# Planning the engine order of a two-layer vision kernel among 40 list schedulings, with refitted weights and DMA landing delays

## The chip, the cores and the metric

The kernel runs on one core of a Trainium2 chip. The metric is device microseconds (us) of one execution; a program on several cores would count its slowest. Its engines are TensorE (PE, matmuls; PEld is its weight load), VectorE (DVE), ScalarE (ACT), GpSimd (POOL) and SyncE (SP), which here only issues DMAs. Each works through its own instructions in order and waits for the others by semaphores.

## The reference

The input is x, (8, 192, 64, 64) in float32. Layer 0 is a windowed attention block, layer 1 a Fourier mixer with an MLP:

```python
# layer 0, windows of 8 x 8 pixels, 6 heads of 32
shortcut = layer_norm(xs)                        # over the 192 channels
q, k, v = split(windows(shortcut) @ qkv_w.T + qkv_b)
attn = einsum(l2n(q), l2n(k)) * temperature      # 64 x 64 per window and head
kth = top_k(attn, 16)[0][..., -1:]
attn = softmax(where(attn >= kth, attn, -100) + rpb)
x2 = shortcut + unwindow(attn @ v) @ proj_w.T + proj_b
x2 = x2 + gelu(layer_norm(x2) @ fc1_w.T + fc1_b) @ fc2_w.T + fc2_b
# layer 1
f = fft2(layer_norm(x), norm="ortho")            # per channel, 64 x 64
h = gelu([f.real, f.imag] @ fc1_w.T + fc1_b) @ fc2_w.T + fc2_b
x = x + ifft2(complex(h[0], h[1])).real
out = x + gelu(layer_norm(x) @ mlp1_w.T + mlp1_b) @ mlp2_w.T + mlp2_b
```

## The kernel before, in words

An image (batch) is cut into 8 bands of 512 pixels. The work is written as Python generators, called tasks, one for each piece:

- `front(b, i)`: loads a band (`load_band`, two bands ahead), turns it into token form on PE (`lt`), normalizes, turns it back (`lc`), makes q, k (`pq`) and v (`pv`) and the norms of q and k (POOL power, L771).
- `attention(b, i, hb)`, two per band: scales q and k, scores on PE (`s`, L924), the 16 largest of each row on DVE (L952 to L956), the mask, softmax over POOL, ACT and DVE, then the transposition of the weights. In batch 0 PE does that (`turned_by_pe`); from batch 1 on DVE transposes 32 x 32 blocks and four SP writes to DRAM (L889) and one SP load (L892) do the rest (`turned_by_dma`). Then the product with v on PE (`po`, L997).
- `back(b, i)`: projection (`pp`), residual, and the first MLP (`mlp`): statistics, normalization (`normalized`, L530 on ACT or L535 on DVE), transposition (from batch 1 on by DVE, four SP writes L580 and three SP loads L583 and L585 into `hn`), first product (`mh`, L622 and L635), gelu on ACT (L606), second product (`mo`, L668).
- `forward`, `pointwise`, `inverse`, for each group of 16 channels: the Fourier transform in matmuls (`fa`, `fz`), the pointwise MLP (`fh` L1177, gelu L1160, `fo` L1204) and the transform back (`fb`, `fy`).
- `leave(b, j)`: the second MLP and the store.

A task yields an `op` before each step: the engine, or a choice of engines (`EITHER` is ACT or DVE), an estimated time for each in units of 10 ns, the tile mode of PE or the table of ACT, buffers that it takes (`get`) and gives back (`put`), and what it waits for (`after`). The function `issue` (L33) is a list scheduler. It keeps, while the program is built, a clock for each engine and a time for each free buffer. The tasks lie in streams (`streams`, at the end of the kernel function): 6 for setup, then `front` with 1 task open at a time, `attention` 3, `back` 2, `forward` 1, `pointwise` 2, `inverse` 1, `leave` 2. At each turn `issue` computes the earliest begin for every open task's next step, takes for each engine the step with the smallest `begin + cost + 360 * place - 100 if it frees PSUM` among those that can begin within 15 units of the first, and issues the one of all engines that begins earliest. `place` is the due place of the task in batches. A change of PE's mode costs 20, of ACT's table 130. A result counts on another engine 15 units later, from PE 30, from SP 210; on the same engine at once. DVE is taken in a choice only if it ends 40 earlier than ACT. The instructions of the step are emitted at that moment, so that the order of choices is the order on each engine and on SP's queue. There are 4 PSUM buffers, 7 `h`, 5 `att`, 4 `xt`, 2 `hn`, 3 each of the DRAM buffers `rows` and `turn`.

The lines that set the old clock:

```python
change = {"pe": 20, "act": 130, "dve": 0, "pool": 0, "sp": 0}
arrives = {"pe": 30, "sp": 210}
...
                    if source is not None and source != engine:
                        end += arrives.get(source, 15)
```

Two steps whose weights the prediction uses are `yield op("sp", 220, put="att")` ahead of the four writes of L889 (and of L580), and `yield op("sp", 45, get="att", put="turn")` ahead of the load L892; the loads of `hn` have 130.

Of the kernel before, what the change touches and what calls it, by code (L numbers as in the profile page):

```python
# [28 lines left out]
def op(engine, weight, mode=None, get="", put="", after=None, done=None, put_too=""):  # L29
    return engine, weight, mode, get.split(), (put + " " + put_too).split(), after, done  # L30


def issue(streams, units):  # L33

    change = {"pe": 20, "act": 130, "dve": 0, "pool": 0, "sp": 0}
    arrives = {"pe": 30, "sp": 210}
    clock = {e: 0 for e in change}  # L40
    mode = {e: None for e in change}
    units = {name: [0] * n for name, n in units.items()}
    events = {}
    live = []

    def advance(task, value):
        try:
            found = task["gen"].send(value)
            while not isinstance(found, tuple):

                new = dict(task, gen=found, queue=None)
                live.append(new)
                advance(new, None)
                found = task["gen"].send(None)
            task["op"] = found
        except StopIteration:
            live.remove(task)
            if task["queue"] is not None:
                start(task["queue"])

    def start(queue):
        if queue[0]:
            gen, place = queue[0].pop(0)
            task = {"gen": gen, "queue": queue, "urgency": 360 * place, "last": (None, 0)}
            queue[1] += 1
            task["order"] = (queue[1], len(live), place)
            live.append(task)
            advance(task, None)

    for tasks, width in streams:  # L70
        queue = [list(tasks), 0]
        for _ in range(width):
            start(queue)
    while live:
        best, ready = {}, {}
        for task in live:
            engines, weights, kind, get, put, after, done = task["op"]
            if isinstance(engines, str):
                engines, weights = (engines,), (weights,)
            free = 0  # L80
            deps = [task["last"]] if after is None else after
            deps = [d if d[0] is None or d[0] in change else events.get(d) for d in deps]
            if any(d is None for d in deps):
                continue
            short = False
            for name in set(get):
                n = get.count(name)
                if len(units[name]) < n:
                    short = True
                    break  # L90
                free = max(free, sorted(units[name])[n - 1])
            if short:
                continue
            found = []
            for engine, weight in zip(engines, weights):
                begin = max(clock[engine], free)
                for source, end in deps:
                    if source is not None and source != engine:
                        end += arrives.get(source, 15)
                    begin = max(begin, end)  # L100
                new = kind and mode[engine] and kind != mode[engine]
                cost = change[engine] if new else 0
                found.append((begin + cost + weight, engine, begin, cost, task, weight))

            _, engine, *rest = min(found, key=lambda f: f[0] + 40 * (f[1] == "dve"))
            ready.setdefault(engine, []).append((engine, *rest))
        for engine, found in ready.items():
            first = min(begin + cost for _, begin, cost, *_ in found) + 15
            best[engine] = min(
                [  # L110
                    (
                        begin + cost + task["urgency"] - 100 * ("ps" in task["op"][4]),
                        task["order"],
                        f,
                    )
                    for f in found
                    for _, begin, cost, task, _ in [f]
                    if begin <= first
                ],
                key=lambda v: v[:2],  # L120
            )
        choice = min(best.values(), key=lambda v: (v[2][1], v[:2]))[2]
        engine, begin, change_cost, task, weight = choice
        _, _, kind, get, put, after, done = task["op"]
        for name in get:
            units[name].remove(min(units[name]))
        end = begin + change_cost + weight
        clock[engine] = end
        if kind:
            mode[engine] = kind  # L130
        for name in put:
            units[name].append(end + (150 if engine == "sp" else 15))
        task["last"] = (engine, end)
        if done:
            events[done] = (engine, end)
        advance(task, (engine, end))


@with_exitstack
def kernel(  # L140
# [7 lines left out]

# [66 lines left out]
    make_identity(nc, ident)  # L225
# [274 lines left out]
    def statistics(src, nm):  # L500
# [3 lines left out]
        for j in range(2):  # L504
            yield op("dve", 54 + 42 * j)
            for t in range(2):
                nc.vector.bn_stats(st[:, t, j, :], src(t, j))
# [5 lines left out]
    def normalized(to, pair, src, mv, nm):  # L513

        yield op("pool", 130)
# [8 lines left out]
        for j in range(2):  # L524
            done = yield op(EITHER, (72, 96), after=[shifted])
# [32 lines left out]
    def mlp(src, nm, w1, fc1_bias, w2, by_dma, then=None):  # L558
# [7 lines left out]
        if by_dma:  # L566
            ready = yield op("dve", 115, get="att rows", put="xa", after=last)
# [7 lines left out]
            yield op("sp", 220, put="att")  # L575
# [5 lines left out]
            yield op("sp", 130, get="hn", put="rows")  # L581
# [7 lines left out]
        else:  # L589
# [3 lines left out]
            done = yield op(EITHER, (80, 96), put="ps")  # L593
# [4 lines left out]
        def gelu(fp, ph, last):  # L598
            yield op("act", 138, "gelu", put="ps", after=[last], done=("gelu", nm, fp))
# [59 lines left out]
        for half in range(2):  # L659
            if half == 0:  # L660
                yield op("pe", 384, "full", get="ps", after=last)
                acc = psum(f"mo_{nm}")
            else:
                last = yield op("pe", 384, "full", put="h h h")
# [16 lines left out]
    def front(b, i):  # L681
# [16 lines left out]
        done = yield op(EITHER, (80, 96), put="ps")  # L698
# [13 lines left out]
        for part in range(2):  # L712
            weights = (100, 100) if part else (62, 67)
# [29 lines left out]
        def squares(p, pq):  # L743
            copied = yield op(EITHER, (80, 96), put="ps")
            copy(copied, qk[:, :, p, :], pq[:, :, : 2 * C])
            squared = yield op(("act", "pool"), (81, 150), get="xa")
# [5 lines left out]
            yield op("dve", 95, put="xa", done=("sq", b, i, p))  # L752
# [23 lines left out]
        def values(whole):  # L776
            done = yield op(EITHER, (80, 96), put="ps", after=[whole], done=("vv", b, i))
            copy(done, vv.rearrange("p t a c -> p t (a c)"), pv[:, :, : 2 * C])
# [77 lines left out]
    def turned_by_pe(s, nm):  # L856
# [11 lines left out]
        moved = yield op(EITHER, (80, 96), put="ps")  # L868
# [4 lines left out]
    def turned_by_dma(s, nm):  # L873
# [3 lines left out]
        yield op("dve", 108, get="att turn", put="att")  # L877
# [6 lines left out]
        yield op("sp", 220, put="att")  # L884
# [16 lines left out]
    def attention(b, i, hb):  # L901

        nm = f"{b}_{i}_{hb}"
        scaled = yield op(("pool", "dve"), (195, 140), after=[("front", b, i, hb), "rpb"])
# [13 lines left out]
        yield op("pe", 55, "s", get="ps ps att", put="qkt")  # L918
# [13 lines left out]
        for k in range(2):  # L932
            done = yield op(EITHER, (49, 56), put="ps")
# [9 lines left out]
        for k0 in range(0, 12, 2):  # L943
            yield op("dve", 100, get="sm" if k0 == 0 else "")
# [12 lines left out]
        yield op("dve", 106)  # L957
        mask = small(shape, "mask", U8)
        nc.vector.tensor_tensor(mask, s, top[:, :, :, 15:16].to_broadcast(shape), ALU.is_lt)
        yield op("dve", 108)  # L960
        nc.vector.copy_predicated(s, mask, row(neg.unsqueeze(1).to_broadcast([128, 3, 4])))  # L961

        yield op("pool", 150)
        nc.gpsimd.tensor_tensor(s, s, top[:, :, :, 0:1].to_broadcast(shape), ALU.subtract)  # L964
        yield op("pool", 190)
        nc.gpsimd.tensor_tensor(s, s, rpb.unsqueeze(2).to_broadcast(shape), ALU.add)
        yield op("act", 85, "exp")
        nc.scalar.activation(s, s, AF.Exp)
        yield op("dve", 117)
# [3 lines left out]
        yield op("pool", 150, put="sm")  # L973
# [7 lines left out]
        if hb == 0:  # L981
            yield op("pe", 53, "v", get="ps ot", put="att", after=[moved, ("vv", b, i)], done=("ot", b, i))
            ots[b, i] = strip("ot", 2, f"ot_{nm}")
        else:
            yield op("pe", 53, "v", get="ps", put="att " + held[b, i][1], after=[moved, ("ot", b, i)])
# [18 lines left out]
        done = yield op(EITHER, (72, 72), put="ps", done=("att", b, i, hb))  # L1004
# [10 lines left out]
    def back(b, i):  # L1015
# [28 lines left out]
        yield op("dve", 98, put="ps", after=[last, ("xt", b, i)])  # L1044
# [5 lines left out]
        def biased():  # L1050
            yield op("pool", 183, done=("biased", b, i))
# [5 lines left out]
        if i > 0:  # L1057
# [3 lines left out]
            98,  # L1061
# [19 lines left out]
        yield op("pool", 200, done=("in", b, i))  # L1081
# [9 lines left out]
    def forward(b, n):  # L1091

        nm = f"{b}_{n}"
        yield op("pool", 250, get="xf", after=[("in", b, i) for i in range(NB)] + ["layer1"])
# [9 lines left out]
        yield op("pe", 90, "full", get="ps fa", put="xf")  # L1104
# [9 lines left out]
        yield op("dve", 70, put="ps")  # L1114
# [11 lines left out]
        yield op("pe", 100, "row32", get="ps ps fz", put="fa")  # L1126
# [13 lines left out]
        for k in range(2):  # L1140
            yield op("dve", 43 + 33 * k, put="ps", done=("fz", b, n) if k else None)
# [10 lines left out]
    def pointwise(b, n, half):  # L1152
# [4 lines left out]
        def gelu(hf, k, ph):  # L1157
            yield op("act", 111, "gelu", put="ps", done=("fh", nm, hf, k))
# [3 lines left out]
        for hf in range(2):  # L1162
            yield op(
                "pe",
                86,
# [21 lines left out]
        if half == 1:  # L1187
# [3 lines left out]
            172,  # L1191
# [142 lines left out]
    with tc.manual_schedule():  # L1334
        issue(streams, units)
# [80 lines left out]
```

## Time and profile before

| | us |
|---|---|
| runs shown (three) | 4822.05, 4823.49, 4830.06; median 4823.49 |
| the profiled execution, its own time | 4827.91 |
| its span, first to last instruction | 4826.1 |
| mean granted clock of PE | 0.963 |
| ACT busiest line: L1160, gelu of the pointwise MLP, 768 times | 813.3 |
| DVE: L952, L954, L956, the search of the 16 largest | 255.8, 309.5 and 125.2, 265.3 |
| POOL busiest line: L771, a power, 128 times | 557.1 |
| DMA moved | 246.42 MB, 51 GB/s on average |

Busy times are unions of the instructions' spans. "a <- b" in a list of waits reads: engine, tile and line that waited, then what ended the wait, the time in total, the number of waits and the longest. SPq is the queue of SP. In a group, "busy, mean ns of one" stand ahead of the bar, idle time of the engine after it. The chain that ended last is put to 66% on PE, 10% on DVE, 7% on POOL, 7% on DMA, 5% on ACT.

### The profile page before, as it was taken

The numbers are of one execution on the slowest core, as the hardware profiler recorded it, in microseconds if no ns is written. First come the engines' busy times: TensorE is split into PE (matmuls) and PEld (weight loads), VectorE is DVE, ScalarE is ACT, GpSimd is POOL, SyncE is SP. The second block draws the span as 40 slices with busy tenths as digits, with TensorE's granted clock in tenths as the row PEclk, the third lists the DMA queues.
The fourth block names the chain that finished last, engine by engine and source line by source line (L and its number), as shares of the span: only waits on it lengthen the run. The fifth ranks groups of instructions, "written<-read, shape, count | busy, mean of one in ns | idle before, by whom it ended". The sixth has DMA issues, their size and how long they took to land.

```text
span 4826.1 us, 143829 instructions
## 1 busy us (share of the span) xinstructions
PE 4441.2 (92%) x60506; PEld 3512.4 (73%) x60506; DVE 2695.8 (56%) x10965; ACT 2542.1 (53%) x3769; POOL 2358.2 (49%) x2188
## 2 busy tenths in 40 slices
PE   6787998999999999899999999999989999999989
PEld 5675766876778766687677876787767877778758
DVE  6776655546665555646665546646476565662111
ACT  4455655346564556445564455644566355652553
POOL 6667545345554455444554455545465465551200
PEclk7888999999999999999999999999999999999999
DMA  2001111221123111222112211122111221121002
GB/s 57 11 8 37 54 32 54 72 61 48 37 59 85 53 41 44 61 73 57 42 46 72 70 48 41 54 67 80 31 48 46 78 70 38 54 63 53 13 15 66
DMA packets 271072, 246.42 MB, mean 51 GB/s; under 512 B 39983, under 2 KB 223482, under 8 KB 270426
## 3 DMA queue, kind: packets, MB, share of 16 engines
q1 hardware_dynamic: 270414, 237.22, 17.7%
q8 instruction: 476, 7.80, 0.7%
q14 instruction: 170, 1.39, 0.1%
q10 hardware_dynamic: 12, 0.00, 0.0%
HBM read 120.52 MB, written 116.39 MB: 49 GB/s over the span
## 4 chain that ended last, share of the span: by engine, by line
PE 66%; DVE 10%; POOL 7%; DMA 7%; ACT 5%; issue 3%; SPq 2%; DVEq 0%; ACTq 0%; POOLq 0%
PE mo_d L668 8%; PE mo_b L668 7%; PE mh_b L622 7%; PE mh_d L622 6%; PE fh L1177 6%; PE fo L1204 6%; PE mh_b L635 3%; PE mh_d L635 3%; PE pq L787 3%; POOL nrm L771 3%; DMA at<-ar 3%; ACT fh L1160 2%; DMA ar<-tt 2%; PE fy L1252 2%; PE fb L1225 2%
## 5 line engine op out<-in xcount | busy, mean ns | idle before, releaser
L1160 ACT ACTIVATE fh<-fh,ab 128x1024 f32<-128x1024 f32 x768 | 813.3, 1110 | 347.0 <-PE fh L1177 344.7
L771 POOL TENSOR_TENSOR nrm<-nrm,mhalf 128x24 f32<-128x24 f32 x128 | 557.1, 4352 | 10.7
L964 POOL TENSOR_TENSOR s<-s,top 128x768 f32<-128x768 f32 x128 | 191.5, 1496 | 720.6 <-DVE s L961 559.5
L668 PE MATMUL mo_b<-wfc,h_b 128*128 128x192 f32 x3072 | 520.5, 328 | 1.0 <-ACT fh L1160 0.5
L668 PE MATMUL mo_d<-wmlp,h_d 128*128 128x192 f32 x3072 | 515.5, 328 | 0.0
L668 PEld LDWEIGHTS mo_b<-wfc,h_b 128*128 128x128 f32 x3072 | 497.8, 190 | 17.4 <-issue 10.7
L668 PEld LDWEIGHTS mo_d<-wmlp,h_d 128*128 128x128 f32 x3072 | 500.5, 190 | 12.7 <-issue 9.6
L1177 PE MATMUL fh<-fz,w1p 32*128 32x264 f32 (+1 forms) x6144 | 468.6, 410 | 14.7 <-ACT fh L1160 6.5
L622 PE MATMUL mh_b<-hn_b,wfc_a 128*128 128x256 f32 x1536 | 391.3, 402 | 34.8 <-DMA hn_b<-lr_b 20.3
L1177 PEld LDWEIGHTS fh<-fz,w1p 32*128 32x128 f32 x6144 | 295.3, 189 | 149.9 <-issue 84.3
L1204 PE MATMUL fo<-fh,w2p 128*32 128x264 f32 (+1 forms) x6144 | 390.9, 389 | 5.7 <-ACT fh L1160 5.5
L622 PE MATMUL mh_d<-hn_d,wmlp_a 128*128 128x256 f32 x1536 | 371.1, 390 | 25.8 <-DMA hn_d<-lr_d 23.1
L622 PEld LDWEIGHTS mh_b<-hn_b,wfc_a 128*128 128x128 f32 x1536 | 290.6, 197 | 109.8 <-issue 42.0
L606 ACT ACTIVATE h_d<-mh_d,fcb 128x512 f32<-128x512 f32 x384 | 240.8, 686 | 230.5 <-PE mh_d L635 169.8
L622 PEld LDWEIGHTS mh_d<-hn_d,wmlp_a 128*128 128x128 f32 x1536 | 286.8, 193 | 88.2 <-issue 44.1
L974 POOL TENSOR_TENSOR s<-s,rsum 128x768 f32<-128x768 f32 x128 | 193.9, 1517 | 241.8 <-DVE rsum L972 157.4
L954 DVE MATCH_REPLACE8 s<-top,s 128x64 f32<-128x64 f32 x1536 | 309.5, 209 | 0.0
L1204 PEld LDWEIGHTS fo<-fh,w2p 128*32 128x32 f32 x6144 | 185.3, 111 | 165.3 <-issue 40.0
L952 DVE MAX8 top<-s 128x8 f32<-128x64 f32 x1536 | 255.8, 207 | 70.4 <-ACT s L852 70.0
L606 ACT ACTIVATE h_b<-mh_b,fcb 128x512 f32<-128x512 f32 x384 | 241.3, 690 | 81.9 <-PE mh_b L635 59.4
L1290 DVE TENSOR_TENSOR zt<-mo_d,xy 128x768 f32<-128x768 f32 x64 | 61.3, 957 | 380.1 <-PE mo_d L668 380.1
L956 DVE MAX8 top<-s 128x8 f32<-128x64 f32 x1536 | 265.3, 214 | 0.0
(214 smaller groups left out, 8469.0 us busy)
## 6 DMA issues: line engine op xcount, KB each, us to landing
ar<-tt SPq DMA_DIRECT2D x448, 96.0 KB
at<-ar SPq DMA_DIRECT2D x112, 384.0 KB
lr_d<-lt_d SPq DMA_DIRECT2D x256, 96.0 KB
lr_b<-lt_b SPq DMA_DIRECT2D x224, 96.0 KB
xin<-in_x SPq DMA_DIRECT2D x64, 256.0 KB
hn_d<-lr_d SPq DMA_DIRECT2D x64, 256.0 KB
out<-z SPq DMA_DIRECT2D x64, 256.0 KB
hn_b<-lr_b SPq DMA_DIRECT2D x56, 256.0 KB
```

The source lines that it names most:

```text
L606: nc.scalar.activation(to, of, AF.Gelu, bias=fc1_bias[:, 2 * fp + k : 2 * fp + k + 1],)
L622: nc.tensor.matmul(ph[:, t, k * HALF : (k + 1) * HALF], w1[0][:, f], hn[:, t * HALF : (t + 1) * HALF], start=(first and k == 0), stop=not ...
L635: nc.tensor.matmul(ph[:, t, k * HALF : (k + 1) * HALF], w1[1][rows, f], hn[rows, BAND:ROW], start=(first and k == 0), stop=not first, skip ...
L668: nc.tensor.matmul(acc[:, j, t * C : (t + 1) * C], hs[f // 2][:, f % 2, q * 128 : (q + 1) * 128], w2[:, f, ORDER[t]], start=(f == 0 and t ...
L771: nc.gpsimd.tensor_tensor(nf, nf, mhalf[:, :24], ALU.pow)
L952: nc.vector.max(best[:, 0:8], of)
L954: nc.vector.match_replace(s2, best[:, 0:8], of, -3.0e38)
L956: nc.vector.max(best[:, 8:16], s2)
L974: nc.gpsimd.tensor_tensor(s, s, row(rsum), ALU.mult)
L1160: nc.scalar.activation(hs[hf, k], ph, AF.Gelu, bias=ab[:, 0:1])
L1177: nc.tensor.matmul(phs[k // 2][:, k % 2, cols], w1p[i][rows, hf].rearrange("p h v -> p (h v)"), fz[rows, :] if rhs is None else zu[rows, : ...
L1204: nc.tensor.matmul(po[rows, :] if i == 0 else pou[rows, :, 1 : U - 1], w2p[i][:, hf].rearrange("p a v -> p (a v)"), hs[hf, k // 2][:, k % ...
```

## The change: what it does

The scheduler is split. `program` builds tasks; the kernel calls it first with a dummy (`Mute`) that swallows every instruction, and `listed` runs all tasks through once, in order of place, and notes for each step its engines, weights, buffers and predecessors. `Plan` then schedules this list with the old rules (same key, the same 15 units, the same 40 on DVE, the same places), and `search` does it in steps: from each state it runs 40 schedules over 40 us, the first without noise, the others with a normal noise of 25 units (0.25 us) added to each step's key; the one with the most work (PE's time counted in full, that of other engines by 0.15) is run for 20 us, and so on. The real program is then issued in the order found. A task may no longer pass the one before it in its stream at the same step (`front`). The clock's constants and the weights are set anew, and a step on SP that follows one on SP now waits for 145.

```diff
-    change = {"pe": 20, "act": 130, "dve": 0, "pool": 0, "sp": 0}
-    arrives = {"pe": 30, "sp": 210}
+CHANGE = {"pe": 19, "act": 128, "dve": 0, "pool": 0, "sp": 0}
+ARRIVES = {"pe": 22, "dve": 18, "act": 15, "pool": 11, "sp": 265}
...
+    def wake(self, task):
...
+            for d in waits:
+                source = self.engine[d]
+                end = self.end[d] + (ARRIVES[source] if source != engine else 145 * (source == "sp"))
+                if end > begin:
+                    begin = end
...
+    def run(self, until, noise=None):
...
+                a = front[task]
+                if a is not None and at[a] <= at[task]:
+                    continue
...
+                        end = begin + cost + weight + (40 if engine == "dve" else 0)
...
+                    key = begin + cost + place[task] - (100 if "ps" in put else 0)
+                    if noise:
+                        key += noise(number)
...
+    def search(self, tries=40, step=2000, horizon=4000, spread=25):
+        draw = random.Random(1)
+        now = 0
+        while self.ready:
+            now = max(now, self.clock["pe"])
+            kept, best = self.save(), None
+            for k in range(tries):
+                seed = draw.random()
+                noise = drawn(seed, spread) if k else None
+                if not self.run(now + horizon, noise):
+                    self.restore(kept)
+                    continue
+                worth = 0
+                for _, _, engine, begin, weight in self.log[kept[-1]:]:
+                    part = min(weight, max(0, now + horizon - begin))
+                    worth += part if engine == "pe" else 0.15 * part
+                if not self.ready:
+                    worth = 1e9 - max(self.clock.values())
+                if best is None or worth > best[0]:
+                    best = worth, seed if k else None
+                self.restore(kept)
+            seed = best[1]
+            self.run(now + step, drawn(seed, spread) if seed is not None else None)
+            now += step
...
+def issue(streams, plan):
+    tasks = Tasks(streams)
+    for name, engine, number in plan:
+        tasks.advance(name, (engine, number))
...
+    streams, units = program(Mute(), Mute(), x, out, w)
+    ops, of_task, made = listed(streams, units)
+    plan = Plan(ops, of_task, made, units, [width for _, width in streams]).search()
+    streams, _ = program(ctx, tc, x, out, w)
+    with tc.manual_schedule():
+        issue(streams, plan)
```

The weights that were changed and matter most, in units of 10 ns:

| step | before | after |
|---|---|---|
| copies out of PSUM, 768 wide, ACT or DVE | 80 or 96 | 69 or 87 |
| normalization, two instructions, ACT or DVE | 72 or 96 | 89 or 58 |
| gelu L1160, one instruction | 111 | 100 |
| gelu L606, two instructions | 138 | 115 |
| scaling of q and k, POOL or DVE | 195 or 140 | 148 or 98 |
| two rows of the search of the 16 largest, DVE | 100 | 90 |
| copies of `po`, ACT or DVE | 72 or 72 | 42 or 54 |
| statistics, first half, DVE | 54 | 50 |
| POOL steps of the softmax | 150, 190, 150 | 157, 177, 144 |
| half of `mo`, PE | 384 | 390 |
| scores `s`, product `po`, PE | 55, 53 | 61, 62 |
| four writes on SP | 220 | 200 |
| loads of `hn` on SP | 130 | 100 |

The computation, its instructions apart from the choices of engine, the buffers and the streams stay.

## The prediction

> **What bounds the kernel now.** I read the page's busy table first, then the windows of 200 us, then the waits of PE by stretch, then those of SP, then single lines and a piece of the timeline.
>
> ```profile
> PE 4441.2 (92%) x60506; PEld 3512.4 (73%) x60506; DVE 2695.8 (56%) x10965; ACT 2542.1 (53%) x3769; POOL 2358.2 (49%) x2188
> ```
>
> PE is the bound. No other engine is above 56%, so the order of work matters only by what it does to PE: its idle time (4826.1 - 4441.2 = 385 us) and what is wasted inside its busy time. The windows tell where the idle time lies (columns: window, its length, busy us of PE, PEld, DVE, ACT, POOL with instructions, PE clock, DMA share, GB/s).
>
> ```profile
> 0.00:200.00 200.00, 140.65 (x1504) 104.75 (x1505) 140.48 (x596) 85.26 (x148) 129.35 (x117) 0.79 0.17 38
> 200.00:400.00 200.00, 162.70 (x1806) 132.24 (x1806) 145.46 (x674) 102.03 (x178) 145.84 (x126) 0.86 0.05 12
> ...
> 1800.00:2000.00 200.00, 171.76 (x2933) 125.49 (x2926) 123.10 (x518) 112.89 (x155) 104.31 (x92) 0.93 0.15 42
> 2000.00:2200.00 200.00, 197.60 (x1690) 172.72 (x1690) 109.72 (x464) 85.69 (x144) 85.09 (x85) 0.99 0.26 72
> ```
>
> The first 400 us lose 97 us; there only batch 0's attention and first MLP exist, and DVE and POOL, at 70%, feed PE. The full stretches lose 2 to 28 us in 200. Summed from the trace by what ended each PE wait: 118 us before 600 us, 227 us from 600 to 4400, 29 us after. Of the 227, DMA ended 119.5, ACT 40.6, DVE 37.0, the sequencer ("issue") 27.7, others 2.2. The waits of PE in that middle stretch:
>
> ```profile
> PE po L997 <- DMA at<-ar: 92.2, 49, 4.6
> PE mh_b L622 <- DMA hn_b<-lr_b: 17.4, 10, 4.6
> PE fb L1235 <- issue: 14.8, 15, 1.6
> PE mh_d L622 <- DMA hn_d<-lr_d: 9.9, 8, 2.6
> ```
>
> So half of PE's idle time in the body is spent behind two matmuls whose operand SP still has on its way (49 waits of 1.88 us, 18 of 1.52 us). PE is in order, so everything planned behind them stands too. That the planner thinks SP faster than it is shows in SP's own waits:
>
> ```profile
> SPq L892 <- DMA ar<-tt: 164.7, 192, 3.2
> SPq L583 <- DMA lr_d<-lt_d: 106.7, 100, 3.5
> SPq L583 <- DMA lr_b<-lt_b: 92.4, 86, 3.1
> ```
>
> The load waits for the landing of the write that stands right before it, which the old planner prices at nothing, since both are on SP.
>
> **The change, part by part** (planner units are 10 ns: half an output product is 24 matmuls, whose usual start-to-start in the trace is 163 ns, 3.91 us; weights 384 and now 390).
>
> (a) Landing delays. Old chain from the transposed tile to `po`: write 220, load 45, arrival 210: 4.75 us. New: 200 + 145 + 45 + 265 = 6.55 us, 1.80 later. For `hn`: 220 + 130 + 210 = 5.60, now 200 + 145 + 100 + 265 = 7.10, 1.50 later. The trace's waits above are 1.88 and 1.52: the correction is almost exactly the error. The records behind it: SP released 1.46 us after the last write's issue ended (24 cases), `po` 2.86 us after its load's (53), `mh` 2.39 after its load's (22). If PE has something else ready for these slots, the waits of L997 and L622 go: 92.2 + 17.4 + 9.9, with 6.9 of `po` before 600 us and 2.9 after 4400, 129 us. If nothing is ready, PE idles just as long: 0. Up to 12 tasks of seven streams (and their sub-tasks) are open at a time and PE was busy in 94% of the middle, so I take three quarters: -95. What is late next is the `ACT` and `DVE` group, 78 us. What stands behind a load on SP (writes of other tasks, `xin` loads, `out`) now waits by plan, not by surprise; SP issues for only 919 us in all, so I count nothing there.
>
> (b) Weights. The timeline shows what they now count:
>
> ```profile
> 2610.21 3.58 ACT L606 ACTIVATE h_d<-mh_d,fcb 128x512 f32<-128x512 f32 x6
> ```
>
> Six activations in 3.58 us are 0.597 each, though their mean is 0.686 in the groups: one begins before the last has ended. The pair weight goes from 138 to 115. Likewise the 128x1024 gelu, 1.110 in the groups and 1.011 from start to start, goes from 111 to 100, and copies from 80 to 69 (0.695 start to start). The new set agrees with start-to-start times within some 2%, the old with durations. A truer clock means fewer PE instructions placed before their operand or after it. Of the 78 us on ACT and DVE I take a quarter, -20. Bounds: -60 and +40 (tighter plan, those waits grow by half).
>
> (c) Choice among 40 schedules. Each 20 us step is tried 40 times over 40 us with noise of 0.25 us on the keys, and the one with the most PE work (0.15 of the others') is kept. Changes of PE tile mode are no work, so they lose. I count 2,018 in the trace's order of matmuls. Across one, start to start is about 0.306 us; usual steps are 0.216 (256 columns), 0.163 and 0.109, so one costs 0.09 to 0.20, and I take 0.14, the 192-column step, the commonest: 283 us in all. A tenth fewer gives -28, rounded to -30. Bounds: +14 (5% more) and -70 (a quarter fewer).
>
> (d) The first 600 us, 118 us of idle, 50 of it POOL: `at` behind `s` 48.6 us. Here latency bounds, not order, but which of three attentions goes first is order. I take -20; bounds +20 and -60 (half).
>
> (e) Normalizing weights go from ACT 72, DVE 96 to 89, 58; with DVE's handicap of 40 it is now taken when ACT is 9 units late (before 64). Today 522 of 768 run on ACT. Should 200 more go, DVE gains 200 x 0.29 = 58 us beside its 2696, ACT loses 200 x 0.44 = 88: hidden under PE. But these are the ones that POOL can hold up:
>
> ```profile
> L535 DVE TENSOR_SCALAR xa_b<-xt,mv_b,rs_b x86: 306/374/1981, 172.3 to 4428.7; 128x192 f32<-128x192 f32 x86
> ```
>
> Of 246 such instructions 19 took 0.74 to 1.98 us, each lying over one POOL instruction to its end: an extra 1.2 us each, 19/246 x 200 x 1.2 = 19 us more on DVE, unplanned. On PE's path I count 0, at worst +15. The Trainium skill's GPSIMD Engine Reference, section 1 (Specifications), speaks against this shift: GpSimd shares SBUF interfaces with VectorE and contends with its two-port instructions. By it each of the 200 could meet POOL, busy 49%, at 1.2 us each, 118 us of DVE; the rows show 8%, not 49%, so the sum stays with the rows.
>
> (f) A later task of a stream may no longer overtake an earlier one at the same step: 0; it only fixes the order that the places already give.
>
> **Sum**: -95 - 20 - 30 - 20 = -165. Against the profiled execution, 4827.9 (span 4826.1 and 1.8 around it): 4662.9. The median of the runs, 4823.5, lies 4.4 lower: **4659**. All bounds together would give 4504 (-319) to 4912 (+89).
>
> **Rivals.**
>
> *Nothing fills the slots.* The new plan puts `po` 1.8 us later and PE idles by plan instead of by wait, because its other work hangs on the same chains. For it: 1800 to 2000 us loses 28 us with DVE, ACT and POOL at 62% or less, so there PE lacked ready work. Against: 2000 to 2200 loses 2.4. With (a) at a quarter, -32, and (c) at half, -15, and the rest: 4737. It holds 4715 to 4813.
>
> *The search finds more.* It also picks schedules by what they make of whole stretches. Should PE idle in the middle halve (-114), the start give -60 and a quarter of the mode changes go (-70): 4823 - 244 = 4580. The granted clock would help: 0.93 where 28 us were idle, 0.99 where 2.4 were. The Trainium skill's TensorE: Matmul & The Clock Gate, Part 1, has the clock halved after about 3.4 us without work; the waits of (a) are shorter, so by the page filling them raises no clock. It holds below 4600.
>
> *Slower: the plan has no slack left.* The old weights put some 0.1 us of reserve on each ACT and DVE result: `fo` was planned 1.11 + 0.15 after its gelu began, now 1.00 + 0.15, and the gelu takes 1.11 by itself, 0.04 of margin. All engines are in order, so each small miss (a POOL collision, a granted clock under 1) stands on PE. By the code there are some 2,970 planned PE steps; a mean extra stall of 0.08 us gives +238, less the 95 of (a) and 50 of (c) and (d): +93, 4916. It decides from 145/2970 = 0.05 us per step. Against it: `fh` behind `ACT fh` waits 0.36 us, but 16 times in 384, and stalls shift later work too, so they don't add one to one. It holds above 4833.
>
> *The plan does not do what it says.* The order is fixed by the planner's clock; if the chip strays from it by more than the noise of 0.25 us within one 40 us horizon, the choice among 40 is a lottery and only (a) and (b) are left: 4823 - 115 = 4708. That lies at the edge of the forecast and is counted half there, half with the first rival.
>
> **Chances.** Forecast (4600 to 4715) 0.50; nothing fills 0.21; more 0.14; within 0.2% 0.04; slower 0.11. 0.2%, some 10 us, is about what a measurement of this kernel can tell from no change. Faster by more 0.85, same 0.04, slower 0.11. The range leaves out the slower case and the lower half of the third (0.07): **4575 to 4813**.
>
> **What would show each step.** (a): `po` behind `DMA at<-ar` falls from 99.1 us under 40 in all, and `mh` behind `hn` under 20. If those fall and PE's busy share stays at 92%, the first rival holds. (b): PE waits on ACT and DVE under 78 us in the middle; above 120 the slower rival holds. (c): fewer than 1,900 changes of tile mode, and PE's busy time below 4441. (d): the first 600 us of the windows more than 481 us busy. (e): more than 246 at L535's successor, with some of them over 1.2 us. The prediction is wrong if PE's idle time moves into waits that no SP chain has, or if the whole program only gets through the start faster.

## The result, and the profile after

The changed kernel takes 4669.61 us (median of 4 runs, 4656.83 to 4674.24) against 4826.77 for the kernel before beside it: a ratio of 0.967, 95% interval 0.9648 to 0.9693, 157 us less. 4659 was predicted. The profiled execution took 4674.24, its span is 4672.5, 153.6 less than before's.

The page's busy table, and the same windows as before (PE, PEld, DVE, ACT, POOL, PE clock, DMA share, GB/s):

```profile
PE 4401.0 (94%) x60506; PEld 3481.1 (75%) x60506; DVE 2738.3 (59%) x11037; ACT 2515.1 (54%) x3704; POOL 2364.3 (51%) x2195
```

```profile
0.00:200.00 200.00, 139.81 (x1570) 105.26 (x1570) 145.55 (x632) 83.53 (x148) 133.42 (x116) 0.81 0.17 39
200.00:400.00 200.00, 181.28 (x2074) 148.98 (x2072) 155.41 (x700) 112.92 (x199) 166.46 (x146) 0.95 0.07 19
...
1800.00:2000.00 200.00, 193.13 (x2810) 148.79 (x2808) 126.54 (x525) 119.56 (x167) 119.54 (x107) 0.99 0.21 59
2000.00:2200.00 200.00, 195.00 (x1852) 166.30 (x1852) 95.09 (x382) 80.23 (x131) 61.13 (x70) 0.98 0.23 65
```

PE has the same 60,506 matmuls, is busy 40 us less and idle 113 us less. The second window does 2,074 of them where it did 1,806, and its clock is 0.95, not 0.86. PE's waits from 600 to 4400 us, and SP's own:

```profile
PE po L1181 <- DMA at<-ar: 22.6, 16, 3.4
PE mh_d L806 <- DMA hn_d<-lr_d: 17.9, 16, 2.3
...
PE fb L1419 <- issue: 6.1, 6, 1.6
...
PE mh_b L806 <- DMA hn_b<-lr_b: 4.0, 5, 1.2
```

```profile
SPq L1076 <- DMA ar<-tt: 124.0, 136, 3.4
...
SPq L767 <- DMA lr_b<-lt_b: 84.6, 83, 3.3
...
SPq L767 <- DMA lr_d<-lt_d: 56.5, 73, 2.8
```

`po` waited 92.2 us here and now 22.6, `mh` 27.3 and now 21.9. SP still waits for the landings, 265 us against 364: that wait is still there, but PE stands behind it less often.

**Where PE's 40 busy us went.** The clock records have two values, full and half, and the pieces at half are 3.4 us long or a multiple of it, but for the last one. Before, the clock stood at half for 354 us, 254 of them with PE busy; after, for 207 and 145. Work at half clock takes twice its time (neighbouring products of L622 start 0.427 us apart there and 0.216 at full clock, medians in the kernel before), so 109 us less of it saves 55. Taking half of the busy time at half clock off gives PE's busy time at full speed: 4314 before, 4329 after, and 4319 to 4343 in the twelve kernels below. So everywhere the span is some 4330 + idle time + half of the busy time at half clock. For the change: -113 idle, -55 clock, +14 rest.

How a short wait costs clock can be seen in the timeline of PE in the kernel before:

```profile
2138.69 1.46 PE L622 MATMUL mh_d<-hn_d,wmlp_a 128*128 128x256 f32 x6
2142.41 1.04 PE L997 MATMUL po<-at,vv 64*32 64x64 f32 x64 [2.26 <-DMA at<-ar]
2143.38 3.21 PE L622 MATMUL mh_d<-hn_d,wmlp_a 128*128 128x256 f32 x8
```

and, of the same kernel, eight matmuls of the same shape without a wait ahead of them:

```profile
2652.48 1.89 PE L622 MATMUL mh_b<-hn_b,wfc_a 128*128 128x256 f32 x8
```

PE stands 2.26 us behind `at`; the clock goes to half 0.06 us after that wait and stays there for 3.41 us. The eight products take 3.21 us where 1.89 is usual, so the wait cost 2.26 us and 1.32 us on these products.

### The profile page after: what moved, and what is told of

Same layout as the page of the kernel before. It is cut to its first block, busy times and chain, and to the rows that moved or that the text cites. A ratio compares the mean times of both kernels' runs of the same rounds, so it can differ in the third digit from the quotient of the medians.

```text
span 4672.5 us, 143843 instructions
## 1 busy us (share of the span) xinstructions
PE 4401.0 (94%) x60506; PEld 3481.1 (75%) x60506; DVE 2738.3 (59%) x11037; ACT 2515.1 (54%) x3704; POOL 2364.3 (51%) x2195
## 5 line engine op out<-in xcount | busy, mean ns | idle before, releaser
L852 PE MATMUL mo_b<-wfc,h_b 128*128 128x192 f32 x3072 | 530.4, 331 | 9.5 <-issue 7.3
L852 PEld LDWEIGHTS mo_b<-wfc,h_b 128*128 128x128 f32 x3072 | 504.0, 192 | 24.0 <-issue 13.6
L806 PE MATMUL mh_b<-hn_b,wfc_a 128*128 128x256 f32 x1536 | 379.9, 392 | 13.4 <-ACT hn_b L1036 4.0
L701 POOL TENSOR_SCALAR rs_d<-mv_d 128x4 f32<-128x4 f32 x64 | 15.4, 240 | 574.9 <-DVE mv_d L694 555.3
L1136 DVE MAX8 top<-s 128x8 f32<-128x64 f32 x1536 | 256.2, 208 | 65.7 <-ACT s L1036 65.5
```

The source lines that it names most:

```text
L806: nc.tensor.matmul(ph[:, t, k * HALF : (k + 1) * HALF], w1[0][:, f], hn[:, t * HALF : (t + 1) * HALF], start=(first and k == 0), stop=not ...
L852: nc.tensor.matmul(acc[:, j, t * C : (t + 1) * C], hs[f // 2][:, f % 2, q * 128 : (q + 1) * 128], w2[:, f, ORDER[t]], start=(f == 0 and t ...
L1136: nc.vector.max(best[:, 0:8], of)
```

## The experiments

Ratios are to the kernel before on the same chip. Per profiled execution: PE's idle time, its busy time at half clock, and its waits behind `at` and `hn`, all in us. A plan made without the search is called plain here.

| kernel | ratio (95%) | idle | half clock | `at` | `hn` |
|---|---|---|---|---|---|
| before | 1 | 385 | 254 | 99 | 43 |
| the change | 0.967 (0.9648 to 0.9693) | 271 | 145 | 33 | 37 |
| landing_only | 0.9784 (0.9763 to 0.9805) | 292 | 166 | 15 | 38 |
| plain_old | 0.9971 (0.9959 to 0.9984) | 358 | 217 | 54 | 38 |
| plain_free | 0.9969 (0.9958 to 0.9979) | 355 | 205 | 54 | 34 |
| no_search | 0.9912 (0.9894 to 0.9929) | 351 | 198 | 74 | 46 |
| no_landing | 0.9793 (0.977 to 0.9815) | 304 | 160 | 73 | 45 |
| seed2 | 0.9703 (0.9681 to 0.9724) | 271 | 104 | 30 | 38 |
| old_weights | 0.9637 (0.9617 to 0.9657) | 262 | 118 | 52 | 39 |
| old_seed2 | 0.9626 (0.9605 to 0.9647) | 254 | 119 | 29 | 50 |
| chain_old | 0.9566 (0.9543 to 0.9588) | 226 | 108 | 9 | 26 |
| sp_reserve | 0.9619 (0.9604 to 0.9634) | 246 | 98 | 7 | 28 |
| norm_old | 0.9625 (0.961 to 0.964) | 236 | 103 | 16 | 32 |
| chain_norm | 0.9635 (0.9619 to 0.9652) | 259 | 130 | 21 | 54 |

Theory A was the prediction's: the landing delays carry most of the gain. Theory B: the search does. Theory C: the weights do.

**landing_only**, in the kernel before:

```diff
-    arrives = {"pe": 30, "sp": 210}
+    arrives = {"pe": 30, "sp": 265}
...
                         end += arrives.get(source, 15)
+                    elif source == "sp":
+                        end += 145
...
-            yield op("sp", 220, put="att")
+            yield op("sp", 200, put="att")
-            yield op("sp", 130, get="hn", put="rows")
+            yield op("sp", 100, get="hn", put="rows")
...
```

> The kernel before with its old scheduler, no search and the old weights; only SP's clock is new: 145 between two steps on SP, arrival 265 for 210, writes 200 for 220, loads of hn 100 for 130. Theory A (the stalls behind SP's loads were the largest loss): `po` behind `at<-ar` falls from 99 us to under 40 and the time by 60 to 100 us, about 4740. Theory B (the search among schedules is the source): the DMA stalls fall, but the time only by 0 to 40 us, about 4805, since PE then idles elsewhere.

Measured 4718.73 (0.9784), 100 us less: theory A, it seemed.

**no_search**: `tries=40` becomes `tries=1` in the changed kernel.

> The changed kernel with one try in place of 40: new weights and landing delays, planned by the plain list schedule. Theory A: landing and weights keep 100 to 120 us of the 157, about 4715. Theory B: it keeps under 60 us, above 4770. Theory C (the weights are the source): about 4690, within 25 us of the changed kernel.

Measured 4779.21 (0.9912), 39 us less than before: theory B. With the landing delays counted, `po` waits again, as the waits of PE in no_search show:

```profile
PE po L1181 <- DMA at<-ar: 74.1, 39, 12.7
```

**no_landing**, in the changed kernel:

```diff
-..., "pool": 11, "sp": 265}
+..., "pool": 11, "sp": 210}
...
-(ARRIVES[source] if source != engine else 145 * (source == "sp"))
+(ARRIVES[source] if source != engine else 0)
```

with SP's weights back at 220 and 130.

> The changed kernel with SP's old clock (nothing between two steps on SP, arrival 210, weights 220 and 130), search and new weights kept. Theory A: the DMA stalls come back (over 110 us of PE behind `at` and `hn`) and the time rises by 60 to 100 us, about 4745. Theory B: the search fills most of it; rise of 0 to 35 us, about 4690.

Measured 4723.82 (0.9793), 1.2 points above the change: about 59 us, and 43 above seed2. The stalls come back (73 + 45 = 118 us, theory A had over 110); the rise lies between the 35 us of theory B and the 60 of theory A.

**old_weights**: the 49 changed lines with weights of PE, ACT, DVE and POOL as before, `CHANGE` and the other arrivals as before.

> The changed kernel with the old weights of PE, ACT, DVE and POOL and their old arrival and mode costs; landing delays and search kept. Theory A: rise of 10 to 35 us, about 4690. Theory C (the refitted weights are the source, since the search is only worth what its clock is): rise of 70 us or more, above 4740.

Measured 4646.68 (0.9637): not slower at all, but 16 us (0.33 points) faster, though the two intervals touch. Both theories had it slower and fall here; so does step (b), if seed2 and old_seed2 bear it out.

**plain_old**: old_weights with one try. Its planning rules, weights and delays are those of landing_only.

> The rewritten scheduler with one try in place of 40, the old weights of PE, ACT, DVE and POOL, and the new landing delays. It differs from landing_only in the rewrite alone (no overtaking in a stream, order of ties) and from no_search in the weights alone. If the new weights cost the 60 us between landing_only (4719) and no_search (4779): about 4720. If the rewrite costs them: about 4780.

Measured 4802.8 (0.9971), 84 us above landing_only, and above both figures that were expected. The two programs issue the same order on ACT, DVE and POOL for the first 888 us; from there on their orders part. Their windows, landing_only's and then plain_old's:

```profile
0.00:800.00 800.00, 672.03 (x9542) 513.95 (x9542) 535.86 (x2291) 436.41 (x672) 516.71 (x448) 0.90 0.13 35
800.00:4400.00 3600.00, 3467.26 (x46888) 2759.19 (x46888) 2092.66 (x8489) 1984.69 (x2930) 1805.38 (x1690) 0.99 0.21 58
```

```profile
0.00:800.00 800.00, 669.79 (x9542) 512.48 (x9542) 543.43 (x2306) 436.86 (x674) 516.48 (x452) 0.90 0.13 35
800.00:4400.00 3600.00, 3404.90 (x46127) 2701.36 (x46128) 2102.46 (x8463) 1935.87 (x2838) 1793.35 (x1668) 0.98 0.20 57
```

The same 9,542 matmuls in 800 us, then 761 fewer in 3600 us. A single list schedule is one draw from a wide lot. The 100 us of landing_only are therefore no measure of the landing delays.

**plain_free**: plain_old without the rule against overtaking.

```diff
-            for a, b in zip(tasks, tasks[1:]):
-                self.front[b] = a
+            pass
```

> plain_old (one try, old weights, new landing delays, 4803) with the rule taken out that a task may not pass the one before it in its stream at the same step. If that rule is what the rewritten scheduler lost against landing_only (4719): 4710 to 4740. If the loss lies elsewhere (the order of ties): 4780 to 4810.

Measured 4795.36 (0.9969, plain_old 0.9971), with the same order on ACT, DVE and POOL to the end: in this plan the rule binds nowhere. What is left between plain_old and landing_only is which of two steps with equal keys goes first: their planners first choose differently at 860.75 us of the planned clock, between two POOL steps whose keys are the same. It also shows how well a ratio repeats.

**seed2** and **old_seed2**: `random.Random(2)` in the changed kernel and in old_weights.

> The changed kernel with another seed of its random numbers. If the search's gain is what the 40 tries do on average, 4655 to 4685. Theory N (much of what lies between these kernels is the luck of one plan): further than 20 us from 4670, and then the 23 us between new and old weights show nothing.

> old_weights with the other seed. If the old weights are better with a search too: 4635 to 4660, under seed2 by 10 us or more. Theory N: within 10 us of seed2 or above it.

Measured 4672.18 (0.9703) and 4635.99 (0.9626). With the search, two plans of the same rules lie 0.1 to 0.3 points apart, where two plain ones lay 1.9 apart. The old weights win with both seeds, by 0.33 and 0.77 points; the first of these is no more than what another seed does.

**chain_old**, in the changed kernel, the steps of `attention` only:

```diff
-scaled = yield op(("pool", "dve"), (148, 98), ...)
+scaled = yield op(("pool", "dve"), (195, 140), ...)
-            yield op("dve", 90, get="sm" if k0 == 0 else "")
+            yield op("dve", 100, get="sm" if k0 == 0 else "")
...
```

and 98, 97, 157, 177, 75, 112, 144 and 96 back to 106, 108, 150, 190, 85, 117, 150 and 108.

> The changed kernel with the old weights of the steps of an attention task alone, from the scaling of q and k to DVE's transposition ahead of SP: 1.2 to 1.7 us more planned for a chain at whose end PE waits for `at`. Theory S (the old weights were a reserve for what the plan does not know, needed at the end of this long chain): PE's wait behind `at<-ar` falls under 25 us and the time by 10 to 30 us, about 4650. Theory P (the shift of normalizations to DVE, where POOL holds them up): no change, 4660 to 4680, since those weights stay new.

Measured 4606.69 (0.9566), the fastest of all. The wait behind `at` falls as theory S has it, but the gain over the change is 1.04 points, about 50 us, where that theory had 10 to 30. PE's waits in it:

```profile
PE mh_d L806 <- DMA hn_d<-lr_d: 23.0, 10, 13.7
...
PE po L1181 <- DMA at<-ar: 9.4, 11, 3.3
```

**sp_reserve**: `"sp": 265` becomes `"sp": 385` in the changed kernel.

> The changed kernel with SP's arrival at 385 in place of 265: 1.2 us of reserve, put at the very end of the chains, where PE waits, and no weight of the attention steps changed. Theory S (a reserve ahead of PE is what chain_old gave): PE's wait behind `at<-ar` falls under 15 us, that behind hn under 30, and the time to 4610 to 4645. Theory D (what helped in chain_old is that DVE and POOL steps are planned at the length they have when they hang on each other): the wait behind `at` falls, but the time stays at 4655 or more.

Measured 4628.52 (0.9619), as theory S has it, in one plan. The wait behind `at` falls too when the reserve stands at the end of the chain and no weight is changed:

```profile
PE po L1181 <- DMA at<-ar: 6.9, 7, 1.9
```

**norm_old**: `(89, 58)` of the normalizations back to `(72, 96)` in the changed kernel.

> The changed kernel with the old weights of the normalizations alone (ACT 72, DVE 96 for 89, 58): fewer than 270 of 768 go to DVE, and fewer of them are held up by POOL than the 48 there. As predicted (hidden beside PE): 4655 to 4685. Theory P (the shift to DVE delays the chains that PE waits for): 4655 or less, by 15 us or more.

Measured 4627.98 (0.9625), 0.45 and 0.78 points under the change and seed2, as theory P has it. DVE takes 286 of 768 (the change 332; under 270 was expected), and 32 of them are held up (48). But chain_old, with 338 on DVE and 45 held up, and sp_reserve, with 372 and 54, beat the change as well, so the number held up does not decide the time.

**chain_norm**: chain_old with norm_old.

> chain_old (4607) with the old weights of the normalizations as well. Theory S alone (a reserve ahead of PE's waits for SP is what counts, and chain_old has it already, with 9 us left behind `at`): 4590 to 4620. If the reserve and the share of ACT and DVE in the normalizations are two separate losses, they add: 4545 to 4585. Above 4630 if both gains were the luck of single plans.

Measured 4655.66 (0.9635): above 4630, and 0.7 points worse than chain_old. The two don't add. So of chain_old's lead over the other plans with a reserve (0.9566 against 0.9619 to 0.9637), and of norm_old's gain, some part is the luck of a plan, and the runs don't tell how much.

## Why the prediction was right, and where it was not

The time came within 11 us of 4669.61, but the terms did not come as they were priced, and that it came so close is partly luck.

(a) *Landing delays, -95.* The error of the old clock was read rightly: `at` and `hn` together fell from 142 to 70 us, -72. Nearly all of that is `at` (99 to 33); `hn` went from 43 to 37, where under 20 was the sign. Two things in the step failed. It counted a landing delay as something that works alone; but plain plans with it came out anywhere from 0.9784 to 0.9971, and behind `at` they waited 15 to 74 us. With the search, taking it out costs 43 to 59 us, one plan against two. And it counted idle time only, while the longer of these waits cost clock as well: of the 67 behind `at` and `hn` from 600 to 4400 us, 23 lasted 2 us or more, and 20 of these brought the clock to half. One `hn` wait of 13.6 us remains at the end; the sum had left out its like before, 13.3 us.

(b) *Weights, -20; bound +40.* The sign was wrong, as far as a few plans can show. PE's waits on ACT and DVE from 600 to 4400 us fell by 10 us (78 to 68), which was the sign asked for. But with the search the old weights give 0.9637 and 0.9626, the new 0.9670 and 0.9703: +27 us on the mean. The three plans that take back only some of the new weights (chain_old, norm_old and chain_norm, 0.9566 to 0.9635) lie under both new ones too. Without the search the one new plan is the better one, 0.9912 against 0.9971, a step smaller than the lot of plain plans is wide.

The step's reading, that start-to-start times are the truer clock and make PE wait less, is where it failed. PE's waits on ACT and DVE from 600 to 4400 us are 68 and 61 us with the new weights and the search, 41 and 49 us with the old ones, which are longer than start to start and so leave a reserve. Behind `at` and `hn` it is the other way: 70 and 68 us with the new weights, 90 and 79 with the old. So the old weights do not gain at the end of the SP chains; chain_old and sp_reserve do, where the wait behind `at` fell from 33 to 9 and 7 us.

One reason why a weight can be too short is argued, not shown: in a chain the next step needs the result. From the mask to the predicated copy, where the one follows the other on DVE without idle time, start to start is 0.993 us at the median and 1.105 on the mean (90 cases in the changed kernel), against 0.98 planned now and 1.06 before; the sum over exponentials and its reciprocal take 0.986 + 0.228 = 1.21, against 1.12 now and 1.17 before. These two come to some 0.2 us of a chain, and sp_reserve changed none of these weights and gained 0.5 to 0.8 points. So the runs speak for a reserve ahead of PE; what it covers stays open.

(c) *Choice among 40, -30 by fewer mode changes.* The effect is there, the mechanism is not: 2,016 changes of tile mode against 2,018. What the search removes is idle time (351 to 271 from no_search to the change) and PE's work at half clock (198 to 145). Between no_search and the two seeds lie 2.1 to 2.4 points, about 100 to 117 us, and the eight searched plans with the landing delays all lie below the three plain plans that have them (plain_free has the plan of plain_old). With the search on, taking out the landing delays costs about half of that, 43 to 59 us. So the search is the larger part of the gain: it picks from the lot where a plain schedule takes the first draw.

(d) *Start, -20.* The term was too small. PE's waits before 600 us fell from 118 to 89 us in all, and its work at half clock there from 102 to 62 us, which saves another 20: some 49 us in all. PE's wait for `at` behind POOL's `s` fell from 48.6 to 21.3. This is the search's doing: by PE's busy time in the windows, PE is idle there for 83 to 98 us in the nine searched plans, and for 113 to 119 in the kernel before and the four plain ones.

(e) *Normalizations to DVE, 0 (at worst +15).* 86 more went to DVE, not 200 (332 against 246), and 48 of them took over 0.45 us, against 19; in the changed kernel:

```profile
L719 DVE TENSOR_SCALAR xa_d<-xy,mv_d,rs_d x160: 306/374/1975, 880.5 to 4638.7; 128x192 f32<-128x192 f32 x160
L719 DVE TENSOR_SCALAR xa_b<-xt,mv_b,rs_b x106: 308/373/1966, 155.0 to 4152.8; 128x192 f32<-128x192 f32 x106
```

That is 51 us of held-up DVE, 14% of the instructions, more than the 8% before and far from POOL's 51% share. Whether PE pays for it stays open: norm_old says yes, but chain_norm, with 264 on DVE and 26 held up, is slower than chain_old with 338 and 45.

(f) *No overtaking, 0.* Shown by plain_free for a plain plan; with the search it was not tested.

**The term that was missing is the clock**, -55 us. The prediction drew on the Trainium skill's TensorE: Matmul & The Clock Gate, Part 1, by which the waits of (a), at 1.9 us, were too short to cost clock, and put the clock into a rival. The measurement decides against that reading: in the kernel before, of the 34 waits of PE of 2 us or more after 600 us, 29 saw a piece at half clock begin, during the wait or within 3.4 us after it, and so did 19 of the 22 among them that were shorter than 3.4 us; of the 15 waits of 1.5 to 2 us it was 3, of the 87 of 0.5 to 1.5 us also 3. Nor were all waits of (a) short: 8 of the 67 were over 3.4 us. Of the -55, some 20 came before 600 us. The -55 made up for what (a), (b) and (c) did not bring; the total was right partly because these errors cancelled.

Of the rivals, *the plan has no slack left* named a mechanism that the runs bear out, at the wrong size: the loss was some 27 us (old weights, mean of two seeds, with shorter waits on ACT and DVE) or 33 us (sp_reserve, 0.9619 against the mean of 0.9670 and 0.9703, with a shorter wait behind `at`), not 0.08 us on each of 2,970 PE steps. *Nothing fills the slots* did not come: PE's busy share rose to 94% and its idle time fell by 113 us. *The search finds more* was right that the search works on whole stretches and that the clock helps, but idle time from 600 to 4400 us fell from 227 to 145 us and not by half. Against *the plan does not do what it says* stands no_search: if the choice among 40 were a lottery, leaving it out would cost nothing.

## What to carry to other kernels

Plan ahead by trying many schedules before refining the clock of one: on this kernel one tie moved a plain plan by 84 us, more than any refinement of its clock was shown to be worth. Judge a planner's constant over several seeds, since one plan proves little. Try a reserve of about a microsecond where a long chain over other engines and DMA ends in front of the engine that bounds the kernel; here sp_reserve gained by it, in one plan.

## What the runs showed of the hardware

- PE's clock mostly goes to half after a single wait of 2 us or more, though the pieces at half are 3.4 us long: 29 of 34 such waits, 19 of the 22 between 2 and 3.4 us, 3 of 87 between 0.5 and 1.5 us. So a wait of 2.26 us cost some 3.6.
- A load on SP's queue that depends on the write ahead of it was released 1.46 us after the write's issue ended; where PE waited for the 384 KB of `at`, it was released 2.86 us after the load's issue ended (medians of 24 and 53 cases, kernel before).
- A DVE normalization that meets a POOL instruction can wait for all of it: up to 1.98 us in place of 0.37. All the held ones, 19 before and 48 after, end some 0.12 us after a POOL instruction does.
